# Adjacency counts of a graph network's first layer: six products in a row instead of four, one-hots asked for two batches ahead

## The chip, the cores and the metric

The kernel runs on one core of one Trainium2 chip. The metric is the device time of one launch in microseconds (us). Three runs of the kernel before gave 2123.55, 2127.40 and 2129.25 us; their median is 2127.4 us.

## The reference

A graph network of four layers over 6250 nodes with 256 channels and 100,000 edges, which come sorted by destination.

```python
h = jnp.maximum(_layernorm(x, axis=-1), 0.0)
# agg(h): for every node, the sum of h[src] over the edges that end in it
def agg(h):
    return jax.ops.segment_sum(h[src], dst, num_segments=N)
# ref(h): three layers of the first form, then the head (256 -> 256 -> 64 -> 256)
for l in range(NL - 1):
    h = x + agg(x)
    h = jax.nn.relu(h @ W1s[l] + b1s[l])
    h = jax.nn.relu(h @ W2s[l] + b2s[l])
    x = h @ W3s[l] + b3s[l]
...
return x + ref(h)
```

The sum over edges is a product with a 6250 x 6250 matrix of counts (how many edges run from node s to node d).

## The kernel before

The nodes lie in 49 blocks of 128. For 19 or so of the destination blocks the sum over edges is made by **gathering**: rows of a table in device memory are fetched by indirect DMAs (`rows`, issued by GpSimd) and added up by TensorE with one-hot matrices (`sums`, L1446). For the other 30 blocks the kernel builds the matrix of counts once, in the first layer, keeps it in device memory as bytes (`mat`), and multiplies with it in every layer: in the first layer `agg` at L1622 takes the counts straight from the build, in the later layers `agg` at L1700 reads them back.

**The build.** A block of 128 destinations is built in two halves of 16 sub-blocks each, so the 30 blocks have 960 sub-blocks. For one sub-block TensorE makes one product, `bp` (L1094), of two one-hot matrices of its edges: `lo` (the source's low seven bits, 128 columns, loaded as weights) and `hi` (the source's block and the destination within the sub-block, 196 columns, streamed). The one-hots are made by VectorE (helper `one_hot`, L1053) for a **batch** of four sub-blocks at a time, `lo` first and then `hi`; the pools hold two `lo` and two `hi` tiles (`bufs=2`). Before that ScalarE spreads the edges' numbers of a half block (`pairs`, L1048). A **step** of the generator `build` makes two products into one of three PSUM tiles `bp` and one copy of both into the block's counts `at`: the odd steps copy on ScalarE (L1102), the even ones on VectorE (L1104). So a batch is two steps: its first copy is ScalarE's, its second VectorE's. At a block's end VectorE adds the identity (L1108) and SyncE stores the block.

**The order of the work.** Instructions go to each engine's queue in the order in which the program writes them, and an engine takes its queue in order. The first 24 steps run before any product with counts. After that the loop `product_by_node` goes through **ticks**. In a tick it first runs what is due (results of the small layers, sums of gathered rows, VectorE's additions `u`, `un`, `zz`, the gathering's one-hots `hot`), then asks the build for some steps, then lets ScalarE cast counts for a later tick (`a`, L1582), and then issues four `agg` products. How many steps a tick asks for stands in a list `goals`, worked out ahead so that 480 steps are spread evenly over the layer:

```python
g0, u1 = GSUB + EARLY, steps - len(node_parts[-1]) - AHEAD - 1
goals = [min(g0 + (total - g0) * u // u1, total) for u in range(1, steps + 1)]
goals = [g - g % 2 for g in goals]
...
goal = min(goals[at - PRE], built[0] + 3)
while built[0] < goal and free_of(built[0] // GSUB - 3):
    next(beside)
    built[0] += 1
```

The goals are about one and a half steps a tick; rounded down to even numbers they come out as none or two steps in a tick. I call what TensorE does for one tick's steps a **piece**: two steps are a piece of four products.

Of the kernel before, what the change touches and what calls it, by code (L numbers as in the profile page):

```python
# [396 lines left out]
def sorted_edges(  # L397
# [55 lines left out]
    BATCH = 4  # L453
# [527 lines left out]
    with tc.manual_schedule():  # L981
# [61 lines left out]
        def pair(hots, k):  # L1043

            if k < len(batches):
                s = batches[k][0]
                pairs[s] = hots.tile([P, 2, GSUB, 2], BF16, name="pairs", bufs=3)
                nc.scalar.copy(pairs[s], clT[:, :, :, s - S0, None].to_broadcast([P, 2, GSUB, 2]))  # L1048

        def one_hot(o, values, which, n):  # L1050

            shape = [P, BATCH, n // 2, 2]
            nc.vector.tensor_tensor(  # L1053
                o.rearrange("p q (n t) -> p q n t", t=2),
                values.rearrange("p (n t) -> p n t", t=2)[:, None, :, :].to_broadcast(shape),
                which[:, :, None, :].to_broadcast(shape), OP.is_equal)

        def low_hot(hots, k):
            if k < len(batches):
                s, q0 = batches[k]  # L1060
                lo = hots.tile([P, BATCH, P], BF16, name="lo", bufs=2)
                one_hot(lo, lanes, pairs[s][:, 1, q0:q0 + BATCH, :], P)
                hot[k] = [lo]

        def high_hot(hots, k):
            if k < len(batches):
                s, q0 = batches[k]
                hi = hots.tile([P, BATCH, HW], BF16, name="hi", bufs=2)
                one_hot(hi, cols, pairs[s][:, 0, q0:q0 + BATCH, :], HW)
                hot[k].append(hi)  # L1070

        def build(hots, ats, ps_b):


            each = GSUB // BATCH
            pair(hots, 0)
            low_hot(hots, 0)
            high_hot(hots, 0)
            step = 0
            for k, (s, q0) in enumerate(batches):  # L1080
                b, half = divmod(s, 2)
                if half == 0 and q0 == 0:
                    at = counts[b] = ats.tile([P, NT, P], U8, name="at", bufs=3)
                lo, hi = hot.pop(k)
                if q0 == 0:
                    pair(hots, k + each)
                for q in range(0, BATCH, 2):
                    if q == 0:
                        low_hot(hots, k + 1)
                    elif q == 2:  # L1090
                        high_hot(hots, k + 1)
                    bp = ps_b.tile([P, W], F32, name="bp")
                    for m in range(2):
                        mm = nc.tensor.matmul(bp[:, m * HW:(m + 1) * HW], lo[:, q + m, :],  # L1094
                                              hi[:, q + m, :], start=True, stop=True)
                    passed(BUILD, mm)
                    d = half * 64 + (q0 + q) * GD
                    o = at[:, :, d:d + 2 * GD].rearrange("p h (i d) -> p h i d", i=2)
                    v = bp[:, :2 * HW].rearrange("p (i h d) -> p h i d", i=2, d=GD)
                    step += 1  # L1100
                    if step % 2 or step <= 2 * PRE:
                        nc.scalar.copy(o, v)  # L1102
                    else:
                        nc.vector.tensor_copy(o, v)  # L1104
                    if half and q0 + q + 2 == GSUB:
                        p, i = place_of[b]
                        own = at[:, b, :]
                        nc.vector.tensor_tensor(own, own, ident, OP.add)  # L1108
                        nc.sync.dma_start(out=mats[p][:, :, i, :],
                                          in_=at.rearrange("p (k h) d -> p k (h d)", h=CH))  # L1110
                    yield
# [449 lines left out]
        def passed(t, ins=None):  # L1561

            clock[0] += t
            if ins is not None:
                paced[:] = [ins.ins.name]
                for g in layers:
                    g.flow()
# [152 lines left out]
        total = GSUB * len(made)  # L1720
        steps = sum(map(len, node_parts))
        g0, u1 = GSUB + EARLY, steps - len(node_parts[-1]) - AHEAD - 1
        goals = [min(g0 + (total - g0) * u // u1, total) for u in range(1, steps + 1)]
        goals = [g - g % 2 for g in goals]
        built = [0]
        late = None
        ahead = ctx.enter_context(tc.tile_pool(name="ahead", bufs=1))
        with tc.tile_pool(name="hots", bufs=1) as hots, tc.tile_pool(
            name="ats", bufs=1
        ) as ats, tc.tile_pool(name="rings", bufs=AHEAD + 2) as rings, tc.tile_pool(  # L1730
            name="gath", bufs=24
        ) as gath, tc.tile_pool(
            name="ps_a", bufs=2, space=PSUM
        ) as ps_a, tc.tile_pool(name="ps_b", bufs=3, space=PSUM) as ps_b:
            begun = {0: clock[0]}
            rings.tile([P, 64], U8, name="align", bufs=1)
            layers[0].begin()
            layers[0].send(8)
            beside = build(hots, ats, ps_b)
            while now[0] < PRE:  # L1740
                for _ in range(2):
                    next(beside)
                    built[0] += 1
                tick(layers[0])
                layers[0].advance()
            later(1, lambda: later(2, lambda bad=verdict(): judge(bad)))
            for team in teams:
                product_of_team(*team, ps_a, beside, team == teams[-1])
            assert next(beside, None) is None and built[0] == total
# [15 lines left out]
def kernel(  # L1765
# [26 lines left out]
    good = keep.tile([1, 1], I32, name="good")  # L1792
    rest = (x, src, dst, W1s, b1s, W2s, b2s, W3s, b3s, cW1, cb1, cW2, cb2, cW3, cb3, out)
    sorted_edges(tc, good, *rest)
    done = nc.values_load(good[0:1, 0:1], min_val=0, max_val=1)
    with tc.If(done == 0):
# [27 lines left out]
```

## Time and profile before

| | |
|---|---|
| median of three runs | 2127.4 us |
| the profiled execution, its own time | 2128.08 us |
| its span, first to last instruction | 2126.3 us |
| TensorE busy / mean granted clock | 2034.3 us (96%) / 0.990 |
| VectorE, ScalarE, GpSimd busy | 925.0, 872.8, 1445.9 us |
| first layer's products with counts and the build beside them | about 134 to 640 us of the span |
| products `bp` | 960, on TensorE for 128.3 us |

The profile comes from one execution that took 2128.08 us by the same clock as the three runs. Times in the rows are in us from the start of the span unless marked ns. A row names line, engine and operation, what is written and read (`out<-in`), how often, and in brackets the idle time just before it with what ended it.

### The profile page before, as it was taken

The numbers are of one execution on the slowest core, as the hardware profiler recorded it, in microseconds if no ns is written. First come the engines' busy times: TensorE is split into PE (matmuls) and PEld (weight loads), VectorE is DVE, ScalarE is ACT, GpSimd is POOL, SyncE is SP. The second block draws the span as 40 slices with busy tenths as digits, with TensorE's granted clock in tenths as the row PEclk, the third lists the DMA queues.
The fourth block names the chain that finished last, engine by engine and source line by source line (L and its number), as shares of the span: only waits on it lengthen the run. The fifth ranks groups of instructions, "written<-read, shape, count | busy, mean of one in ns | idle before, by whom it ended". The sixth has DMA issues, their size and how long they took to land.

```text
span 2126.3 us, 33236 instructions
## 1 busy us (share of the span) xinstructions
PE 2034.3 (96%) x12076; PEld 1495.9 (70%) x12076; DVE 925.0 (44%) x2103; ACT 872.8 (41%) x1793; POOL 1445.9 (68%) x1467
## 2 busy tenths in 40 slices
PE   6889999999999999999999999999999999989998
PEld 4657676667676777777777777777776767766665
DVE  6987767677662422232234322322233323223333
ACT  5766656456555433323233423232233322222222
POOL 3747777677774477777777477777776477777772
PEclk9989999999999999999999999999999999999999
DMA  5534455545455654555566554555555555555563
GB/s 174 159 117 148 145 156 150 157 139 162 140 161 168 205 163 145 160 177 161 154 184 202 171 165 149 176 166 158 169 171 176 173 170 185 161 184 185 154 189 109
DMA packets 184900, 347.54 MB, mean 163 GB/s; under 512 B 32446, under 2 KB 118496, under 8 KB 184726
## 3 DMA queue, kind: packets, MB, share of 16 engines
q0 software_dynamic: 68960, 185.36, 29.9%
q1 hardware_dynamic: 113838, 158.12, 22.8%
q8 instruction: 96, 1.57, 0.3%
q10 hardware_dynamic: 1928, 1.85, 0.3%
q14 instruction: 78, 0.64, 0.1%
HBM read 287.93 MB, written 57.26 MB: 162 GB/s over the span
## 4 chain that ended last, share of the span: by engine, by line
PE 86%; DMA 4%; DVE 3%; issue 1%; ACT 1%; POOL 1%; DVEq 0%; SPq 0%; POOLq 0%; ACTq 0%
PE agg L1700 43%; PE agg L1622 15%; PE sums L1446 11%; PE ps L1256 6%; PE ps L1313 6%; PE bp L1094 4%; DMA rows<-table,idx 4%; PE ps L1506 1%; DVE hi L1053 1%; POOL rows L1407 1%; DVE at L1104 1%; PE ps L1268 1%; PE ps L1248 0%; DVE lo L1053 0%; ACT at L1102 0%
## 5 line engine op out<-in xcount | busy, mean ns | idle before, releaser
L1407 POOL DMA_INDIRECT rows<-table,idx x1394 | 1388.8, 996 | 595.7 <-issue 225.7
L1700 PE MATMUL agg<-a,XY 128*128 128x512 f32 x4116 | 978.6, 395 | 1.9 <-DVE clT L1634 1.9
L1700 PEld LDWEIGHTS agg<-a,XY 128*128 128x128 f32 x4116 | 764.9, 188 | 192.7 <-issue 35.0
L1598 ACT CAST a<-at 128x512 fp32r<-128x512 uint8 (+1 forms) x542 | 328.7, 617 | 653.7 <-PE agg L1700 613.1
L1598 DVE CAST a<-at 128x512 fp32r<-128x512 uint8 x543 | 246.8, 456 | 515.7 <-PE agg L1700 479.1
L1622 PE MATMUL agg<-XY,a 128*128 128x512 f32 x1470 | 405.4, 410 | 1.7 <-ACT a L1582 1.0
L1622 PEld LDWEIGHTS agg<-XY,a 128*128 128x128 f32 x1470 | 260.0, 190 | 51.4 <-issue 6.6
L1446 PE MATMUL sums<-rows,hot 128*32 128x256 f32 x3772 | 248.3, 391 | 33.5 <-DMA rows<-table,idx 33.3
L1446 PEld LDWEIGHTS sums<-rows,hot 128*32 128x32 f32 x3772 | 124.0, 111 | 151.0 <-DMA rows<-table,idx 46.1
L1582 ACT CAST a<-at 128x512 fp32r<-128x512 uint8 (+2 forms) x362 | 197.2, 576 | 6.6 <-PE agg L1622 6.6
L1102 ACT CAST at<-bp 128x392 uint8<-128x392 f32 x252 | 121.5, 490 | 186.9 <-PE bp L1094 181.3
L1104 DVE CAST at<-bp 128x392 uint8<-128x392 f32 x228 | 128.6, 564 | 137.4 <-PE bp L1094 135.0
L1475 DVE TENSOR_TENSOR u<-u,sums 128x256 f32<-128x256 f32 x82 | 34.4, 419 | 301.3 <-PE agg L1700 273.6
L1094 PE MATMUL bp<-hi,lo 128*128 128x196 bf16 x960 | 128.3, 256 | 14.9 <-DVE hi L1053 13.3
L1313 PE MATMUL ps<-w,h 128*128 128x256 f32 x588 | 133.8, 379 | 1.4 <-ACT h L1259 0.9
L1053 DVE TENSOR_TENSOR hi<-cols,pairs 128x784 bf16<-128x784 bf16 x240 | 134.9, 562 | 0.0
L1256 PE MATMUL ps<-h,w 128*128 128x512 f32 (+3 forms) x332 | 133.8, 545 | 0.3 <-ACT h L1713 0.3
L1094 PEld LDWEIGHTS <-lo 128*128 128x128 bf16 x960 | 72.3, 100 | 83.5 <-DVE hi L1053 34.9
L1313 PEld LDWEIGHTS ps<-w,h 128*128 128x128 f32 x588 | 111.3, 190 | 18.5 <-ACT h L1259 1.4
L1321 DVE TENSOR_TENSOR zz<-ps,w 128x512 f32<-128x512 f32 (+1 forms) x75 | 50.2, 679 | 116.5 <-PE ps L1313 116.5
L1053 DVE TENSOR_TENSOR lo<-lanes,pairs 128x512 bf16<-128x512 bf16 x240 | 100.6, 419 | 0.7 <-issue 0.3
L1510 ACT ACTIVATE h<-ps,bias 128x256 f32<-128x256 f32 (+1 forms) x116 | 47.6, 464 | 128.5 <-PE ps L1506 128.5
(170 smaller groups left out, 962.6 us busy)
## 6 DMA issues: line engine op xcount, KB each, us to landing
at<-mat SPq DMA_DIRECT2D x151, 448.0 KB
mat<-at SPq DMA_DIRECT2D x30, 784.0 KB
rows<-table,idx POOLq DMA_INDIRECT x1394
table<-zz SPq DMA_DIRECT2D x72, 256.0 KB
back<-table SPq DMA_DIRECT2D x99, 128.0 KB
xs<-in_x_dram SPq DMA_DIRECT2D x8, 768.0 KB
table<-zs SPq DMA_DIRECT2D x24, 256.0 KB
out_dram<-zz SPq DMA_DIRECT2D x24, 256.0 KB
```

Of the source, the lines that this page charges most:

```text
L1053: nc.vector.tensor_tensor(o.rearrange("p q (n t) -> p q n t", t=2), values.rearrange("p (n t) -> p n t", t=2)[:, None, :, :].to_broadcast( ...
L1094: mm = nc.tensor.matmul(bp[:, m * HW:(m + 1) * HW], lo[:, q + m, :], hi[:, q + m, :], start=True, stop=True)
L1102: nc.scalar.copy(o, v)
L1104: nc.vector.tensor_copy(o, v)
L1256: mm = nc.tensor.matmul(ps[:mp, :w], weights[l][0][:, c, i * P:i * P + mp], h1[:, c, :w], start=(c == 0), stop=(c == KC - 1))
L1313: mm = nc.tensor.matmul(o, h2[0][:, c, nodes], w3[:, c, :], start=(c == 0), stop=(c == KC - 1))
L1407: got = nc.gpsimd.indirect_dma_start(out=t, out_offset=None, in_=tables[self.l][:, :], in_offset=bass.IndirectOffsetOnAxis(ap=idx[:, o:o + ...
L1446: nc.tensor.matmul(self.sums[m * Q:(m + 1) * Q, :C], self.hot[:, c - min(rounds), m, :], self.rows[g, c + 4 * m], start=(c == ROUNDS[0][0] ...
L1582: nc.scalar.copy(a[:, i * m * P:(i + 1) * m * P].rearrange("p (j d) -> p j d", j=m), counts[b][:, j:j + m, :])
L1598: cast(o, at[:, :, d:d + m * P])
L1622: mm = nc.tensor.matmul(agg, a[:, d:d + P], XY[:, j, :], start=(j == 0), stop=(j == NT - 1))
L1700: mm = nc.tensor.matmul(agg[c][:, :w], XY[:, j, o:o + P], a[:, :w], start=(at == 0 and half == 0), stop=(at == NT - 1 and half == 1))
```

## The change

Three edits in the first layer's build. `goals` are rounded down to multiples of three instead of two (the last goal stays the full number), so a tick asks for three steps or none: a piece is six products. The two one-hots of batch k+2 are written behind the second step of batch k, where before those of batch k+1 were written ahead of batch k's first and second step; and the one-hots of the first two batches are written at the start instead of those of the first alone. The pools of `lo`, `hi`, `bp` and `at` keep their sizes. In the changed kernel L1094 is L1091, L1102 is L1099 and L1104 is L1101; L1053 and L1108 keep their numbers.

```diff
             each = GSUB // BATCH
             pair(hots, 0)
-            low_hot(hots, 0)
-            high_hot(hots, 0)
+            for k in range(2):
+                low_hot(hots, k)
+                high_hot(hots, k)
             step = 0
             for k, (s, q0) in enumerate(batches):
                 b, half = divmod(s, 2)
...
                 lo, hi = hot.pop(k)
                 if q0 == 0:
                     pair(hots, k + each)
                 for q in range(0, BATCH, 2):
-                    if q == 0:
-                        low_hot(hots, k + 1)
-                    elif q == 2:
-                        high_hot(hots, k + 1)
                     bp = ps_b.tile([P, W], F32, name="bp")
                     for m in range(2):
                         mm = nc.tensor.matmul(bp[:, m * HW:(m + 1) * HW], lo[:, q + m, :],
                                               hi[:, q + m, :], start=True, stop=True)
                     passed(BUILD, mm)
...
                     step += 1
                     if step % 2 or step <= 2 * PRE:
                         nc.scalar.copy(o, v)
                     else:
                         nc.vector.tensor_copy(o, v)
+                    if q + 2 == BATCH:
+                        low_hot(hots, k + 2)
+                        high_hot(hots, k + 2)
                     if half and q0 + q + 2 == GSUB:
                         p, i = place_of[b]
                         own = at[:, b, :]
                         nc.vector.tensor_tensor(own, own, ident, OP.add)
...
-        goals = [g - g % 2 for g in goals]
+        goals = [g if g == total else g - g % 3 for g in goals]
```

**TensorE's order**, right behind the first 24 steps (`bp`, `lo` and `hi` carry numbers, so that the tiles can be told apart). Before, a piece of four products and the `agg` of one tick:

```order
L1094 LDWEIGHTS lo_1440
L1094 MATMUL bp_1472<-hi_1446,lo_1440 128x196
L1094 LDWEIGHTS lo_1440
L1094 MATMUL bp_1472<-hi_1446,lo_1440 128x196
L1094 LDWEIGHTS lo_1440
L1094 MATMUL bp_1478<-hi_1446,lo_1440 128x196
L1094 LDWEIGHTS lo_1440
L1094 MATMUL bp_1478<-hi_1446,lo_1440 128x196
L1622 MATMUL agg_1453<-XY_71,a_1458 128x512 x4
```

Now the first piece of six there; eight `agg` stand ahead of it and eight behind it:

```order
L1091 LDWEIGHTS lo_1440
L1091 MATMUL bp_1482<-hi_1442,lo_1440 128x196
L1091 LDWEIGHTS lo_1440
L1091 MATMUL bp_1482<-hi_1442,lo_1440 128x196
L1091 LDWEIGHTS lo_1440
L1091 MATMUL bp_1486<-hi_1442,lo_1440 128x196
L1091 LDWEIGHTS lo_1440
L1091 MATMUL bp_1486<-hi_1442,lo_1440 128x196
L1091 LDWEIGHTS lo_1452
L1091 MATMUL bp_1494<-hi_1454,lo_1452 128x196
L1091 LDWEIGHTS lo_1452
L1091 MATMUL bp_1494<-hi_1454,lo_1452 128x196
```

A piece of four used one batch (`lo_1440`); a piece of six uses one and a half, and it fills all three `bp` tiles. The next piece begins with the second half of `lo_1452`. I call a piece that begins with a fresh batch an **A piece** and one that begins halfway a **B piece**; they alternate.

**VectorE's order**, some 410 us into the span, where the gathering's instructions fall between two pieces. Before:

```order
L1104 COPY at<-bp 128x49x8
L1475 TENSOR_TENSOR u<-u,sums 128x256
L1430 TENSOR_TENSOR hot<-colf,rel 128x768
L1634 TENSOR_TENSOR un<-un,agg 128x256
L1053 TENSOR_TENSOR lo<-lanes,pairs 128x512
L1053 TENSOR_TENSOR hi<-cols,pairs 128x784
L1104 COPY at<-bp 128x49x8
```

Now, at the same place:

```order
L1101 COPY at<-bp 128x49x8
L1053 TENSOR_TENSOR lo<-lanes,pairs 128x512
L1053 TENSOR_TENSOR hi<-cols,pairs 128x784
L1108 TENSOR_TENSOR at<-at,ident 128x128
L1475 TENSOR_TENSOR u<-u,sums 128x256
L1430 TENSOR_TENSOR hot<-colf,rel 128x768
L1634 TENSOR_TENSOR un<-un,agg 128x256
L1101 COPY at<-bp 128x49x8
```

The sequence of a batch's copy and the next one-hots (copy, `lo`, `hi`, copy, `lo`, `hi`) is the same in both kernels. What moved is the other work: it stood between a copy and the one-hots behind it, and stands now behind these one-hots and ahead of the next copy.

Counted over the layer behind the first 24 steps, TensorE's order had 224 pieces (216 of four products, 8 of six) and has 156 (148 of six, 4 of four, 4 of two). Between a B piece and the A piece behind it there stand 37 times exactly eight `agg`, 9 times five, and otherwise eight with further work (transposes L1506, the small layers L1256 and L1313, `sums` L1446) or more. The order of the later layers' instructions did not change.

## The prediction

> **What bounds the kernel now.** I read first the busy time by stage, then the chain of work that ended last, then who waited for whom in the first layer, then the timeline of single pieces. The stages (TensorE, its weight loads, VectorE, ScalarE and GpSimd busy, the granted clock, the DMA share):
>
> ```profile
> 121.00:134.00 13.00, 10.01 (x50) 5.48 (x50) 11.84 (x29) 10.42 (x27) 8.44 (x8) 0.50 0.58 192
> 134.00:640.00 506.00, 496.90 (x3356) 350.98 (x3357) 359.43 (x815) 302.79 (x683) 362.88 (x362) 0.99 0.49 148
> ```
>
> The first row is the build of the first 24 steps alone; the second is the stage that the change reorders. TensorE is busy for 496.9 of its 506 us, VectorE for 359, so on average nobody but TensorE binds. The chain says the same of the whole span:
>
> ```profile
> PE 86%; DMA 4%; DVE 3%; issue 1%; ACT 1%; POOL 1%; DVEq 0%; SPq 0%; POOLq 0%; ACTq 0%
> ```
>
> So a change in this stage is worth what it adds to or takes from TensorE's line: its own work, and its waits. The waits of TensorE from 134 to 640 us (total, times, longest):
>
> ```profile
> PE bp L1094 <- DVE hi L1053: 7.2, 12, 1.4
> PE agg L1622 <- ACT a L1582: 1.0, 1, 1.0
> PE ps L1313 <- ACT h L1510: 0.5, 1, 0.5
> PE bp L1094 <- ACT at L1102: 0.3, 2, 0.2
> ```
>
> Nearly all of it is a piece that waits for a one-hot `hi`. These waits are few, twelve of 224 pieces. The longest has VectorE's other work for a cause: behind a copy came `u`, `hot` and `un`, and only then the next one-hots.
>
> ```profile
> 407.82 1.17 PE L1622 MATMUL agg<-XY,a 128*128 128x512 f32 x4
> 410.34 0.26 PE L1094 MATMUL bp<-hi,lo 128*128 128x196 bf16 x1 [1.35 <-DVE hi L1053]
> ```
>
> **What the change can remove.** (1) These waits. Idle time is counted from a matmul's modelled end, but the next matmul may start earlier, so more is lost than the row says. One `agg` has a record of 413 ns, while twelve in a row take 2.79 us, 0.233 us each:
>
> ```profile
> L1622 PE MATMUL agg<-XY,a 128*128 128x512 f32 x1162 | 329.3, 413 | 1.0 <-ACT a L1582 1.0
> 327.71 2.79 PE agg L1622 x12
> ```
>
> Each wait costs 0.413 - 0.233 = 0.18 us more than its idle time. So the one-hots cost 7.2 + 12 x 0.18 = 9.4 us and the wait for ScalarE's copy 0.3 + 2 x 0.18 = 0.7 us. If the one-hots were truly ahead, 10.1 us would go.
>
> (2) Changes between the build's products and `agg`. The timeline has pieces of six and of four side by side, since the kernel before makes a few of six when it catches up:
>
> ```profile
> 438.78 0.67 PE L1094 MATMUL bp<-hi,lo 128*128 128x196 bf16 x6
> 439.24 1.17 PE L1622 MATMUL agg<-XY,a 128*128 128x512 f32 x4
> 440.25 0.34 PE L1094 MATMUL bp<-hi,lo 128*128 128x196 bf16 x2
> 440.76 0.51 PE L1094 MATMUL bp<-hi,lo 128*128 128x196 bf16 x4 [0.16 <-ACT at L1102]
> 441.05 1.18 PE L1622 MATMUL agg<-XY,a 128*128 128x512 f32 x4
> 442.07 0.51 PE L1094 MATMUL bp<-hi,lo 128*128 128x196 bf16 x4
> 442.37 0.48 PE L1622 MATMUL agg<-XY,a 128*128 128x512 f32 x1
> 443.35 0.51 PE L1094 MATMUL bp<-hi,lo 128*128 128x196 bf16 x4 [0.50 <-DVE hi L1053]
> ```
>
> Six products take 439.24 - 438.78 = 0.46 us, four take 0.29 or 0.30. Four `agg` between pieces take 1.01 us instead of 4 x 0.233 = 0.93, so each piece costs 0.08 us beside its products. Twelve products cost 3 x (0.30 + 0.08) = 1.14 us in fours and 2 x (0.46 + 0.08) = 1.08 us in sixes: about 0.05 us saved for each piece less (0.03 with 0.29). There are 224 - 156 = 68 fewer: 3.4 us (2 to 4).
>
> (3) In the first 24 steps VectorE's identity addition waits for ScalarE and holds up a one-hot behind it; it now stands behind that one-hot. The wait there was 0.70 us:
>
> ```profile
> 130.81 1.65 PE L1094 MATMUL bp<-hi,lo 128*128 128x196 bf16 x8 [0.70 <-DVE hi L1053]
> ```
>
> I take 0.5 us of it, between 0 and 0.7. The rest of that phase keeps its sequence.
>
> Together 9.4 + 0.7 + 3.4 + 0.5 = 14.0 us.
>
> **What it adds.** "Two batches ahead" gives less than it says. VectorE's sequence copy, `lo`, `hi`, copy is the same as before, and a batch's one-hots still go into the tiles of the batch two earlier: they cannot begin until that batch's last product is done. What changes is when TensorE wants them. A piece of six eats one and a half batches at once, and a B piece ends two batches. VectorE behind the pieces shown above:
>
> ```profile
> 439.32 0.57 DVE L1104 CAST at<-bp 128x392 uint8<-128x392 f32 x1 [2.26 <-PE bp L1094]
> 439.81 0.41 DVE L1053 TENSOR_TENSOR lo<-lanes,pairs 128x512 bf16<-128x512 bf16 x1
> 440.14 0.56 DVE L1053 TENSOR_TENSOR hi<-cols,pairs 128x784 bf16<-128x784 bf16 x1
> 440.63 0.57 DVE L1104 CAST at<-bp 128x392 uint8<-128x392 f32 x1
> 441.12 0.41 DVE L1053 TENSOR_TENSOR lo<-lanes,pairs 128x512 bf16<-128x512 bf16 x1
> 441.45 0.56 DVE L1053 TENSOR_TENSOR hi<-cols,pairs 128x784 bf16<-128x784 bf16 x1
> 441.93 0.56 DVE L1104 CAST at<-bp 128x392 uint8<-128x392 f32 x1
> 442.40 0.42 DVE L1053 TENSOR_TENSOR lo<-lanes,pairs 128x512 bf16<-128x512 bf16 x1
> 442.73 0.56 DVE L1053 TENSOR_TENSOR hi<-cols,pairs 128x784 bf16<-128x784 bf16 x1
> ```
>
> This is the new rhythm in small. The piece at 438.78 is an A piece: its second step's copy starts 0.54 us after it, and its one-hots let the product at 440.76 go, 1.98 us after it. At 440.25 products of the B kind begin (half a batch, then a batch). VectorE's copy starts 0.38 us after them; copy, `lo`, `hi` take 1.30 us, then the second copy, `lo`, `hi` follow without a break, and the product that needs the second `hi` starts at 443.35: **3.10 us after the B piece began.** Nothing else stood in VectorE's queue there and the copy cannot start before its products end, so 3.10 is a floor.
>
> When does TensorE want it? It is the second batch of the next A piece, its fifth product. The fifth starts 0.35 us into a piece (the last two of the six, from 439.13 on), and eight `agg` between two others take 311.28 - 309.34 = 1.94 us:
>
> ```profile
> 439.13 0.33 PE L1094 MATMUL bp<-hi,lo 128*128 128x196 bf16 x2
> 309.34 2.10 PE L1622 MATMUL agg<-XY,a 128*128 128x512 f32 x8
> 311.28 0.38 PE L1313 MATMUL ps<-w,h 128*128 128x256 f32 x1
> ```
>
> So it is wanted 0.46 + 1.94 + 0.35 = 2.75 us after the B piece began: a **wait of 0.35 us at every A piece that has just eight `agg` ahead of it**, 37 x 0.35 = 13.0 us. Where five `agg` stand there, the time is 3 x 0.233 = 0.70 us shorter and the wait 1.05 us: 9 x 1.05 = 9.5 us. Where a transpose, a small layer or sums stand there too, I take none. From A to B there is slack: the B piece's third product (0.18 us in, half of the fifth's 0.35) comes 0.46 + 1.94 + 0.18 = 2.58 us after the A piece began and its one-hots after 1.98. At four places pieces of two and four come with four `agg` between; there an A piece's one-hots are wanted after 0.46 + 1.01 + 0.18 = 1.65 us: 4 x 0.33 = 1.3 us.
>
> In the wait stand the rest of the piece and all `agg` behind it, so it adds to TensorE's line in full; the next copy waits with it, so the rhythm repeats instead of drifting.
>
> VectorE's other work comes on top where it falls ahead of a B piece. An A and a B piece together take 2 x 2.40 + 0.35 = 5.15 us, and three batches keep VectorE for 3.9 us; 1.25 us are free, enough for one `hot` of 0.95 us:
>
> ```profile
> L1430 DVE TENSOR_TENSOR hot<-colf,rel 128x768 f32<-128x768 f32 x21 | 20.0, 952 | 0.0
> ```
>
> So most of it fits, as it did not in the single batch between two pieces of four. I take 2 us for what does not, between 0 and the 9.4 us that it costs now.
>
> The three `bp` tiles are all filled by a piece; the last copy of a B piece starts 441.93 - 440.25 = 1.68 us after it began, long before 2.75: no wait. The store of a block moves behind two one-hots, under 1 us, ticks before its next use: nothing. The later layers keep their order, and the chain there is TensorE's and the gathering's; what the first layer loses shifts them whole.
>
> **The sum.** Added 13.0 + 9.5 + 1.3 + 2.0 = 25.8 us, removed 14.0: **+11.8 us.** On the profiled execution's 2128.1 us that is 2139.9; the median of the runs is 0.7 lower: **2139 us.**
>
> A rule of the Trainium skill bears on this ("Perfetto Trace Analysis", Optimization Strategy): the same gap repeating on the engine that should be saturated can mean that no buffer is free for the next tile. By it the repeated wait would be cured by a third pair of `lo` and `hi`, which this change does not bring; the trace shows twelve scattered waits and no regular one, so it has nothing to say of the kernel before.
>
> **The rivals.**
>
> *The one-hots are in time* (faster). Removed 14.0, nothing added: 2113 to 2116. For it: the longest waits now come from work that the change moves behind the one-hots. Against it: the 3.10 us. It wants the eight `agg` at least 0.35 us longer than measured. Chance 0.10.
>
> *Half of the wait is hidden* (no change). If ScalarE's casts `a` hold `agg` back between pieces, as once for 1.0 us in the waits above, the wait for the one-hot falls into that time. With half, 22.5 / 2 + 1.3 + 2.0 - 14.0 = +0.6 us: 2128, with 2124 to 2133 around it. Chance 0.17.
>
> *VectorE falls behind* (slower still). If the 1.25 us are not free when `hot` comes, each of the 21 adds its 0.95 us to a tight piece: 18 us more than I took, 2157. It decides where more than 1.25 us of other work stands ahead of a B piece. Chance 0.10.
>
> *The clock drops* (slower). In the first 24 steps TensorE was busy for 10.0 of 13 us and the granted clock was 0.50; with waits of 1.35 us in the stage behind it was 0.99. If the regular waits took a tenth of the 506 us to half clock, that tenth would last twice as long: +50 us, 2190. TensorE would then idle 0.35 of 5.15 us, far less than the 3 of 13. Chance 0.03. The Trainium skill ("TensorE: Matmul & The Clock Gate", A second HAM failure mode: psum-queue depth-cycling) tells of a kernel whose short idle times between groups made the clock swing between full and half; the trace's 0.99 speaks against it here.
>
> **How the numbers follow.** My forecast has 0.60; its own range is 2132 (waits of eight `agg` at half) to 2147 (other work at its upper bound). The range 2127 to 2150 leaves out the faster rival, the clock, and most of the falling behind, together 0.2. About 0.3%, 6.4 us, is what a measurement can tell from no change. Slower by more: 0.60 less a tenth of it, and 0.13, and a little of the half-hidden case: 0.69. Within: 0.20. Faster: 0.11.
>
> **What would show it.** Right: in the changed profile an idle of some 0.2 us (0.35 less 0.18 or so) in front of a piece's last two products, by `hi`, about every second piece, and 3.1 us from a B piece to them; `bp`'s idle by `hi` well above 7.2 us; waits of over 1 us rarer than before. Wrong: pieces of six without a break, or a stage from 134 us on that ends before 640; or waits that ScalarE's copies end.

## The result and the profile after

The changed kernel takes 2140.93 us (median of six runs, 2135.43 to 2143.27), the kernel before beside it 2126.97 us (six runs, 2123.44 to 2129.34): a ratio of 1.0064, 95% interval 1.0048 to 1.0081. That is 14.0 us slower; the forecast was +11.8 us, 2139. In the changed kernel the copies of a step stand at L1099 (ScalarE) and L1101 (VectorE) and the build's product at L1091. Not used below are one execution of the fifth experiment (2287.86 us, granted clock 0.848) and two single executions, 2400.78 us for the changed kernel and 2391.22 for the one before, from a chip on which all of them, a further one of the kernel before at 2377.9 included, took some 12% longer.

The chain of work that ended last, in the changed kernel, shares of the span by engine:

```profile
PE 81%; DVE 8%; DMA 4%; issue 1%; ACT 1%; POOL 0%; DVEq 0%; SPq 0%; POOLq 0%; ACTq 0%
```

VectorE has 8% of the chain instead of 3%, and TensorE 81% instead of 86%: the chain now leaves TensorE at many places and goes through VectorE. TensorE's waits from 134 to 655 us in the same execution (total, times, longest):

```profile
PE bp L1091 <- DVE hi L1053: 16.4, 47, 0.8
PE agg L1622 <- ACT a L1582: 1.0, 1, 1.0
PE ps L1506 <- ACT h L1259: 0.5, 1, 0.5
PE bp L1091 <- ACT at L1099: 0.3, 2, 0.2
```

Twelve scattered waits for `hi` have become 47, and none is over 0.8 us. Two pieces of the timeline, TensorE first (start, duration, instructions, and in brackets the idle time ahead and who ended it), with eight `agg` and with five between them:

```profile
144.11 0.69 PE L1091 MATMUL bp<-hi,lo 128*128 128x196 bf16 x6
144.58 2.09 PE L1622 MATMUL agg<-XY,a 128*128 128x512 f32 x8
146.51 0.52 PE L1091 MATMUL bp<-hi,lo 128*128 128x196 bf16 x4
147.21 0.34 PE L1091 MATMUL bp<-hi,lo 128*128 128x196 bf16 x2 [0.18 <-DVE hi L1053]
...
149.27 0.69 PE L1091 MATMUL bp<-hi,lo 128*128 128x196 bf16 x6
149.73 1.40 PE L1622 MATMUL agg<-XY,a 128*128 128x512 f32 x5
151.08 0.51 PE L1091 MATMUL bp<-hi,lo 128*128 128x196 bf16 x4
152.37 0.34 PE L1091 MATMUL bp<-hi,lo 128*128 128x196 bf16 x2 [0.77 <-DVE hi L1053]
```

And VectorE in the same timeline:

```profile
144.50 0.57 DVE L1101 CAST at<-bp 128x392 uint8<-128x392 f32 x1 [1.02 <-PE bp L1091]
144.98 0.41 DVE L1053 TENSOR_TENSOR lo<-lanes,pairs 128x512 bf16<-128x512 bf16 x1
145.31 0.56 DVE L1053 TENSOR_TENSOR hi<-cols,pairs 128x784 bf16<-128x784 bf16 x1
145.79 0.56 DVE L1101 CAST at<-bp 128x392 uint8<-128x392 f32 x1
146.26 0.42 DVE L1053 TENSOR_TENSOR lo<-lanes,pairs 128x512 bf16<-128x512 bf16 x1
146.60 0.56 DVE L1053 TENSOR_TENSOR hi<-cols,pairs 128x784 bf16<-128x784 bf16 x1
...
150.46 0.56 DVE L1053 TENSOR_TENSOR hi<-cols,pairs 128x784 bf16<-128x784 bf16 x1
```

The B piece at 144.11 runs without a break. VectorE, which had waited 1.02 us, starts its copy 0.39 us after it and then works copy, `lo`, `hi`, copy, `lo`, `hi` without a break; the product that needs the second `hi` starts at 147.21, **3.10 us after the B piece began**. The next B piece at 149.27 and its product at 152.37: again 3.10.

The stage from 134 us on (TensorE, its weight loads, VectorE, ScalarE, GpSimd busy, granted clock, DMA share), and the first and last start of the first layer's and the later layers' `agg` (durations min/median/max, then the two starts), after:

```profile
134.00:655.00 521.00, 502.93 (x3371) 356.88 (x3371) 357.90 (x816) 304.08 (x691) 363.07 (x365) 1.00 0.49 146
```

```profile
L1622 PE MATMUL agg<-XY,a x1470: 387/395/793, 134.6 to 1938.9; 128*128 128x512 f32 x184
L1700 PE MATMUL agg<-a,XY x4116: 387/389/796, 702.2 to 2131.1; 128*128 128x512 f32 x196
```

The same two rows of the kernel before:

```profile
L1622 PE MATMUL agg<-XY,a x1470: 387/395/799, 134.6 to 1923.5; 128*128 128x512 f32 x184
L1700 PE MATMUL agg<-a,XY x4116: 387/389/793, 690.8 to 2116.0; 128*128 128x512 f32 x196
```

The granted clock in this stage was 1.00. I take the time from the first L1622 to the first L1700 as the first layer's: 702.2 - 134.6 = 567.6 us after, 690.8 - 134.6 = 556.2 before, **+11.4 us**. The span after is 2141.5 us, so what follows takes 1439.3 us, before 2126.3 - 690.8 = 1435.5. Whether these other 3.8 us belong to the change is asked in the last experiment.

### The profile page after: what moved, and what is told of

Read it like the earlier page. It is cut to its first block, busy times and chain, and to the rows that moved or that the text cites. A ratio compares the mean times of both kernels' runs of the same rounds, so it can differ in the third digit from the quotient of the medians.

```text
span 2141.5 us, 33241 instructions
## 1 busy us (share of the span) xinstructions
PE 2040.3 (95%) x12076; PEld 1501.4 (70%) x12076; DVE 920.5 (43%) x2103; ACT 870.8 (41%) x1793; POOL 1444.5 (67%) x1467
## 4 chain that ended last, share of the span: by engine, by line
PE 81%; DVE 8%; DMA 4%; issue 1%; ACT 1%; POOL 0%; DVEq 0%; SPq 0%; POOLq 0%; ACTq 0%
PE agg L1700 42%; PE agg L1622 11%; PE sums L1446 11%; PE ps L1313 6%; PE ps L1256 6%; DMA rows<-table,idx 4%; PE bp L1091 3%; DVE hi L1053 2%; DVE at L1101 2%; DVE lo L1053 2%; PE ps L1506 1%; PE ps L1268 1%; ACT at L1099 0%; PE ps L1248 0%; DVE hot L1430 0%
## 5 line engine op out<-in xcount | busy, mean ns | idle before, releaser
L1700 PE MATMUL agg<-a,XY 128*128 128x512 f32 x4116 | 979.0, 395 | 1.9 <-DVE clT L1634 1.9
L1700 PEld LDWEIGHTS agg<-a,XY 128*128 128x128 f32 x4116 | 765.1, 188 | 193.1 <-issue 35.1
L1622 PE MATMUL agg<-XY,a 128*128 128x512 f32 x1470 | 391.5, 406 | 1.7 <-ACT a L1582 1.0
L1622 PEld LDWEIGHTS agg<-XY,a 128*128 128x128 f32 x1470 | 262.7, 189 | 59.7 <-issue 10.7
L1446 PE MATMUL sums<-rows,hot 128*32 128x256 f32 x3772 | 249.9, 393 | 33.6 <-DMA rows<-table,idx 33.3
L1446 PEld LDWEIGHTS sums<-rows,hot 128*32 128x32 f32 x3772 | 124.7, 112 | 151.9 <-DMA rows<-table,idx 45.9
L1099 ACT CAST at<-bp 128x392 uint8<-128x392 f32 x252 | 119.1, 489 | 191.6 <-PE bp L1091 185.1
L1101 DVE CAST at<-bp 128x392 uint8<-128x392 f32 x228 | 128.3, 563 | 157.9 <-PE bp L1091 154.9
L1582 ACT CAST a<-at 128x512 fp32r<-128x512 uint8 (+2 forms) x362 | 191.0, 576 | 9.2 <-PE agg L1622 9.2
L1091 PE MATMUL bp<-hi,lo 128*128 128x196 bf16 x960 | 124.6, 255 | 23.3 <-DVE hi L1053 21.5
L1313 PE MATMUL ps<-w,h 128*128 128x256 f32 x588 | 135.4, 383 | 0.9 <-ACT h L1259 0.9
L1053 DVE TENSOR_TENSOR hi<-cols,pairs 128x784 bf16<-128x784 bf16 x240 | 134.8, 562 | 0.0
L1256 PE MATMUL ps<-h,w 128*128 128x512 f32 (+3 forms) x332 | 133.8, 545 | 0.3 <-ACT h L1713 0.3
L1091 PEld LDWEIGHTS <-lo 128*128 128x128 bf16 x960 | 71.8, 99 | 82.9 <-DVE hi L1053 39.0
L1313 PEld LDWEIGHTS ps<-w,h 128*128 128x128 f32 x588 | 112.6, 192 | 18.3 <-ACT h L1259 1.3
L1053 DVE TENSOR_TENSOR lo<-lanes,pairs 128x512 bf16<-128x512 bf16 x240 | 100.2, 417 | 0.7 <-issue 0.5
```

Of the source, the lines that this page charges most:

```text
L1053: nc.vector.tensor_tensor(o.rearrange("p q (n t) -> p q n t", t=2), values.rearrange("p (n t) -> p n t", t=2)[:, None, :, :].to_broadcast( ...
L1256: mm = nc.tensor.matmul(ps[:mp, :w], weights[l][0][:, c, i * P:i * P + mp], h1[:, c, :w], start=(c == 0), stop=(c == KC - 1))
L1313: mm = nc.tensor.matmul(o, h2[0][:, c, nodes], w3[:, c, :], start=(c == 0), stop=(c == KC - 1))
L1446: nc.tensor.matmul(self.sums[m * Q:(m + 1) * Q, :C], self.hot[:, c - min(rounds), m, :], self.rows[g, c + 4 * m], start=(c == ROUNDS[0][0] ...
L1582: nc.scalar.copy(a[:, i * m * P:(i + 1) * m * P].rearrange("p (j d) -> p j d", j=m), counts[b][:, j:j + m, :])
L1622: mm = nc.tensor.matmul(agg, a[:, d:d + P], XY[:, j, :], start=(j == 0), stop=(j == NT - 1))
```

## The experiments

The theory: the batch's one-hots are too late by a fixed amount, because VectorE's sequence from a B piece to the second `hi` behind it takes 3.10 us and TensorE wants that `hi` earlier; fours did not have this, and making one-hots earlier cannot cure it with two pairs of tiles. The rivals: sixes alone cost nothing and the new place of the one-hots costs; the tiles alone are short; ScalarE could hide it; the first trace is an odd one.

**Sixes alone** (kernel before with the new goals):

```diff
-        goals = [g - g % 2 for g in goals]
+        goals = [g if g == total else g - g % 3 for g in goals]
```

> Pieces of six products, but the one-hots written where the kernel before writes them (one batch ahead). My theory (the waits come from the piece of six: a B piece ends two batches, and VectorE's copy, lo, hi, copy, lo, hi has its last hi ready 3.10 us after the piece began, while it is wanted after 2.75 us, or 2.05 where five agg stand between): the same waits of 0.35 us and about 1.0 us stay, and other work of VectorE comes between a copy and the one-hots again, so 0 to 6 us slower than the changed kernel, ratio to the kernel before 1.006 to 1.010. Rival (writing the one-hots further ahead is what costs): the loss is gone, ratio 0.997 to 1.001.

Measured 2169.83 us, ratio 1.019 (1.0172 to 1.0208): the direction was right, the size not, it is far slower than the changed kernel. TensorE's waits for `hi` from 134 to 690 us:

```profile
PE bp L1094 <- DVE hi L1053: 41.6, 56, 2.1
```

With 0.18 us more for each that is 41.6 + 56 x 0.18 = 51.7 us instead of 9.4. One such wait in this kernel's timeline, both engines:

```profile
173.15 0.56 DVE L1104 CAST at<-bp 128x392 uint8<-128x392 f32 x1
173.28 0.51 PE L1094 MATMUL bp<-hi,lo 128*128 128x196 bf16 x4
...
173.62 0.41 DVE L1475 TENSOR_TENSOR u<-u,sums 128x256 f32<-128x256 f32 x1
...
173.95 0.95 DVE L1430 TENSOR_TENSOR hot<-colf,rel 128x768 f32<-128x768 f32 x1
...
174.82 0.41 DVE L1053 TENSOR_TENSOR lo<-lanes,pairs 128x512 bf16<-128x512 bf16 x1
175.15 0.56 DVE L1053 TENSOR_TENSOR hi<-cols,pairs 128x784 bf16<-128x784 bf16 x1
...
175.77 0.34 PE L1094 MATMUL bp<-hi,lo 128*128 128x196 bf16 x2 [1.97 <-DVE hi L1053]
```

In the old order the one-hots of a batch are written only when the batch ahead of it starts, that is behind the tick's `u` and `hot`; here these put 174.82 - 173.62 = 1.20 us between the copy and the one-hots, and the wait, already tight, grows by that. It is no single case: in this trace some thirty of the waits have `u`, `hot`, `un` or `zz` in VectorE's line ahead of the `hi`, and they hold about 34 of the 41.6 us. So the two edits do not add up: sixes without the earlier one-hots cost 42 us, and with them 14.

**One-hots ahead alone** (changed kernel with the old goals):

```diff
-        goals = [g if g == total else g - g % 3 for g in goals]
+        goals = [g - g % 2 for g in goals]
```

> Pieces of four products as before, the one-hots written two batches ahead. My theory: the sequence copy, lo, hi is the same and a batch is used at a time, so no regular wait; some of the twelve waits behind u, hot, un, zz go: 0 to 7 us faster than the kernel before, ratio 0.9965 to 1.000, idle of bp by hi 2 to 6 us instead of 7.2. Rival (writing them ahead is what costs, since copies and the identity addition now wait behind them or they hold up u and un): ratio about 1.006.

Measured 2122.77 us, ratio 0.998 (0.9967 to 0.9994), with these waits for `hi` from 134 to 655 us:

```profile
PE bp L1091 <- DVE hi L1053: 5.1, 11, 1.3
```

The earlier one-hots are a small gain by themselves, 4 us by the ratio (1 to 7 by its interval). They do not take the scattered waits away: 5.1 + 11 x 0.18 = 7.1 us of the 9.4 are left, the longest still 1.3 us. There, at 409.41, VectorE had worked `u`, `hot`, `un`, copy, `lo`, `hi` without a break: the other work that stood ahead of the one-hots stands now ahead of the copy, and the one-hots behind that copy are late all the same. The loss is in the sixes.

**Three pairs of tiles, three batches ahead** (changed kernel; two row tiles fewer in the first layer's pool make room):

```diff
-                lo = hots.tile([P, BATCH, P], BF16, name="lo", bufs=2)
+                lo = hots.tile([P, BATCH, P], BF16, name="lo", bufs=3)
...
-                hi = hots.tile([P, BATCH, HW], BF16, name="hi", bufs=2)
+                hi = hots.tile([P, BATCH, HW], BF16, name="hi", bufs=3)
...
-            for k in range(2):
+            for k in range(3):
...
-                        low_hot(hots, k + 2)
-                        high_hot(hots, k + 2)
+                        low_hot(hots, k + 3)
+                        high_hot(hots, k + 3)
...
-            name="gath", bufs=24
+            name="gath", bufs=22
```

> Pieces of six, three lo and three hi tiles, one-hots written three batches ahead; to make room the first layer's gathering has 22 row tiles instead of 24. My theory: in a B piece the one-hots wanted by the next A piece's fifth product now stand behind the first copy, ready 1.82 us after the piece began, wanted at 2.75: the regular waits go, about 22 to 26 us faster than the changed kernel, ratio to the kernel before 0.994 to 0.997. Rival (VectorE simply has too much work in this stage): the waits stay in sum, ratio 1.004 or more. Rival (the loss lies in the later layers): ratio about 1.006.

Measured 2116.11 us, ratio 0.9942 (0.9923 to 0.9961): faster than both kernels. No wait for `hi` is left among the waits from 134 to 655 us; the build's products wait only for ScalarE's copies:

```profile
PE bp L1091 <- ACT at L1099: 1.3, 3, 0.5
```

TensorE's timeline shows A and B pieces alike, unbroken:

```profile
141.10 0.68 PE L1091 MATMUL bp<-hi,lo 128*128 128x196 bf16 x6
141.57 2.11 PE L1622 MATMUL agg<-XY,a 128*128 128x512 f32 x8
143.52 0.68 PE L1091 MATMUL bp<-hi,lo 128*128 128x196 bf16 x6
```

And its first and last starts:

```profile
L1622 PE MATMUL agg<-XY,a x1470: 387/395/797, 133.0 to 1911.8; 128*128 128x512 f32 x184
L1700 PE MATMUL agg<-a,XY x4116: 387/389/796, 677.7 to 2100.2; 128*128 128x512 f32 x196
```

The first layer takes 677.7 - 133.0 = 544.7 us, 11.5 less than before. This is the prediction's faster rival, brought about: it was priced at 2113 to 2116.

**Three pairs, still two ahead** (the same without the three lines that write further ahead):

```diff
-                lo = hots.tile([P, BATCH, P], BF16, name="lo", bufs=2)
+                lo = hots.tile([P, BATCH, P], BF16, name="lo", bufs=3)
...
-                hi = hots.tile([P, BATCH, HW], BF16, name="hi", bufs=2)
+                hi = hots.tile([P, BATCH, HW], BF16, name="hi", bufs=3)
...
-            name="gath", bufs=24
+            name="gath", bufs=22
```

> The changed kernel with three lo and three hi tiles, still two batches ahead, 22 row tiles in the first layer. My theory: the tiles are free when VectorE comes to them, its queue is what is late, so nothing changes: ratio to the kernel before 1.005 to 1.008, the same waits of 0.35 us. Rival (a repeated gap means that no buffer is free for the next tile): the waits go, ratio about 0.995. If 22 row tiles cost something, it shows here too.

Measured 2138.28 us, ratio 1.0046 (1.0029 to 1.0063), which overlaps the changed kernel's interval. Its waits for `hi`, from 134 to 655 us:

```profile
PE bp L1091 <- DVE hi L1053: 15.5, 45, 0.8
```

A free tile alone is worth almost nothing: the batch's one-hots still stand behind the same copy in VectorE's queue, and the copy behind the same products. The rule of the Trainium skill that the prediction weighed ("Perfetto Trace Analysis", Optimization Strategy: a gap that repeats on the engine that should be saturated can mean too few buffers) is half of the answer here: with the third pair but the old order 15.5 us of waits stayed, and only with both were they gone. No cost of the two row tiles given up shows in this run.

**One-hots ahead of the copy** (changed kernel, the same place in the program but in the other order):

```diff
+                    if q + 2 == BATCH:
+                        low_hot(hots, k + 2)
+                        high_hot(hots, k + 2)
                     step += 1
                     if step % 2 or step <= 2 * PRE:
                         nc.scalar.copy(o, v)
                     else:
                         nc.vector.tensor_copy(o, v)
-                    if q + 2 == BATCH:
-                        low_hot(hots, k + 2)
-                        high_hot(hots, k + 2)
```

> The changed kernel with the one-hots of batch k+2 written ahead of the second step's copy instead of behind it. My theory: in a B piece VectorE then goes lo, hi, copy, lo, hi, copy. The second hi lets its product go 2.63 us after the piece began, in time for 2.75, but the last copy ends only some 3.1 us after it, and the next A piece's third step needs that copy's bp tile at 2.75: the wait stays at about 0.35 us and changes its name to VectorE's copy. Ratio to the kernel before 1.003 to 1.008, bp's idle by hi well below the 16.4 us of the changed kernel and by the copy L1104 or its like well above 0. Rival (only the one-hots are late): the 37 waits go, ratio about 1.000.

Measured 2139.65 us, ratio 1.0056 (1.0035 to 1.0076), and the waits from 134 to 655 us (in this kernel L1102 is ScalarE's copy and L1104 VectorE's):

```profile
PE bp L1091 <- ACT at L1102: 8.2, 16, 0.8
PE bp L1091 <- DVE at L1104: 6.4, 28, 0.6
...
PE bp L1091 <- DVE hi L1053: 0.5, 1, 0.5
```

The wait for `hi` is gone and the time stays: the copies that free the three `bp` tiles are now last. With 0.18 us for each of the 45 waits the three rows hold 15.1 + 8.1 = 23.2 us, against 16.4 + 47 x 0.18 = 24.9 in the changed kernel. The same operations in another order are late by about as much, while one operation less, in the next experiment, is not late behind eight `agg`. That ScalarE's copies would be charged with 8.2 of the 15.1 us was not expected. One such wait, in a piece that began at 153.87:

```profile
154.40 0.50 ACT L1102 CAST at<-bp 128x392 uint8<-128x392 f32 x1
154.65 0.56 DVE L1104 CAST at<-bp 128x392 uint8<-128x392 f32 x1
154.94 0.33 PE L1091 MATMUL bp<-hi,lo 128*128 128x196 bf16 x2 [0.56 <-ACT at L1102]
```

The fifth product starts while VectorE's copy still runs, and 0.04 us after the end of ScalarE's, which is the copy of the same piece's first step. All 16 follow the first step's copy in this way. That points to the first step's tile and not, as expected, to the one that the piece before filled last; why the tile would come from there is not shown.

**One copy of three given to ScalarE** (changed kernel; of a batch's VectorE copies, the one of each B piece's first step, whose `lo` and `hi` are the first in the tight sequence):

```diff
-                    if step % 2 or step <= 2 * PRE:
+                    if step % 2 or step % 6 == 4 or step <= 2 * PRE:
```

> The changed kernel with the first copy of every B piece on ScalarE instead of VectorE, so VectorE goes lo, hi, copy, lo, hi there. My theory: the second hi lets its product go 2.63 us after the piece began instead of 3.10: the 37 waits of 0.35 us go and the 9 with five agg fall from 1.05 to about 0.6, 17 us less; ScalarE gets 76 copies of 0.49 us more in a stage where it is busy for 304 of 521 us and gives back up to 5. Ratio to the kernel before 0.997 to 1.002. Rival (ScalarE becomes the bound of the stage): casts a come late, ratio 1.005 or more, agg idle by ScalarE.

Measured 2122.62 us, ratio 0.9989 (0.9976 to 1.0003). The waits from 134 to 655 us, and then the timeline of TensorE:

```profile
PE bp L1091 <- DVE hi L1053: 5.0, 13, 0.7
```

```profile
148.44 2.10 PE L1622 MATMUL agg<-XY,a 128*128 128x512 f32 x8
150.38 0.68 PE L1091 MATMUL bp<-hi,lo 128*128 128x196 bf16 x6
150.85 1.41 PE L1622 MATMUL agg<-XY,a 128*128 128x512 f32 x5
152.09 0.52 PE L1091 MATMUL bp<-hi,lo 128*128 128x196 bf16 x4
153.01 0.34 PE L1091 MATMUL bp<-hi,lo 128*128 128x196 bf16 x2 [0.40 <-DVE hi L1053]
```

One copy less in the 3.10 us (0.48 us from its start to that of `lo`) is enough behind eight `agg`: the piece at 150.38 is whole. Behind five it is not: 153.01 - 152.09 = 0.92 us instead of 0.35, a wait of 0.57. ScalarE took 76 copies more (every sixth step behind the first 24, in which all copies are its own). TensorE waits for it no longer than before: 1.0 us for `a`, 0.5 for `h`, 0.3 for the copies, as in the changed kernel. VectorE's waits for ScalarE rose from 0.7 to 9.4 us, but the total does not show them. So the margin is as computed, a few tenths of a microsecond.

**Three pairs, three ahead, in fours** (the third experiment's kernel with the old goals):

```diff
-        goals = [g if g == total else g - g % 3 for g in goals]
+        goals = [g - g % 2 for g in goals]
```

> Pieces of four, three lo and three hi tiles, one-hots three batches ahead, 22 row tiles in the first layer: the kernel with pieces of six and the same (ratio 0.9942) with only the piece's size put back. My theory: the twelve waits behind other work go (up to 10 us), the saving of the larger piece (68 changes at 0.05 us, 3.4 us) is missing: ratio to the kernel before 0.994 to 0.998, last bp product 2 to 5 us later after the first agg than with sixes. Rival (all the gain of three ahead with sixes comes from the size): ratio 0.999 to 1.001.

Measured 2115.37 us, ratio 0.9943 (0.9924 to 0.9962), the same as in sixes within the intervals. Its starts:

```profile
L1622 PE MATMUL agg<-XY,a x1470: 387/396/797, 132.8 to 1912.3; 128*128 128x512 f32 x184
L1700 PE MATMUL agg<-a,XY x4116: 387/389/792, 680.1 to 2106.5; 128*128 128x512 f32 x196
```

The first layer takes 547.3 us, 2.6 more than in sixes. With no wait for a one-hot in either (the products wait for ScalarE's copies for 1.3 us in sixes and for 0.6 in fours), this is an estimate of what 68 changes between the build's products and `agg` are worth, about 0.04 us each. Since the first layer differs by up to 1.7 us between two traces of one kernel (last experiment), it may be 0.01 to 0.06; the time of the whole run does not show it.

**Second traces of both kernels**, to see what varies between executions (unchanged kernels). The expectations reckon the later layers to an earlier point, 7.0 us before the end: 1432.3 and 1428.5 us for the 1439.3 and 1435.5 above.

> The changed kernel once more, for a second trace that can be compared (the two before this took 12% longer for both kernels). If the 3.8 us of the later layers are the kernel's own, they take 1431 to 1434 us here too; if they differ from execution to execution, any time from 1425 to 1434. The first layer repeats: 567 to 568 us.

> The kernel before once more, for the same comparison: first layer 556 to 557 us; later layers 1428 to 1429 us if what they take is the kernel's own, else any time from 1425 to 1434.

Measured: 2138.59 us, ratio 1.0056 (1.0021 to 1.0092), span 2134.6, for the changed kernel; 2127.24 us, ratio 1.0002 (0.9989 to 1.0016), span 2129.2, for the one before. The starts in the changed kernel's second trace:

```profile
L1622 PE MATMUL agg<-XY,a x1470: 387/394/796, 134.3 to 1933.8; 128*128 128x512 f32 x184
L1700 PE MATMUL agg<-a,XY x4116: 387/389/793, 703.5 to 2124.4; 128*128 128x512 f32 x196
```

And in the second trace of the kernel before:

```profile
L1622 PE MATMUL agg<-XY,a x1470: 387/395/799, 134.1 to 1921.3; 128*128 128x512 f32 x184
L1700 PE MATMUL agg<-a,XY x4116: 387/389/793, 689.6 to 2118.8; 128*128 128x512 f32 x196
```

First layer 569.2 and 555.5 us, 1.2 and 0.5 us outside what was expected: +13.7, against +11.4 in the first pair of traces. What follows it takes 2134.6 - 703.5 = 1431.1 us after and 2129.2 - 689.6 = 1439.6 before, the other way round than at first (1439.3 and 1435.5); by the expectations' count that is 1424.1 and 1432.6, the first just below the 1425 to 1434 that were expected. So the later layers vary by 8 us from execution to execution with the same order, and the 3.8 us of the first trace are that; the loss lies in the first layer.

## Why the prediction was right, point by point

**The floor of 3.10 us** was met to the hundredth, at 147.21 and at 152.37.

**Eight `agg` ahead: 0.35 us.** 147.21 - 146.51 = 0.70 us from the first product to the fifth instead of 0.35: a wait of 0.35. Of the 47 waits 27 are of this kind, in front of a fifth product behind eight `agg` and with 0.15 to 0.19 us of idle time; the forecast had 37. With 0.18 us for each they hold 9.7 us instead of 13.0.

**Five ahead: 1.05 us.** Eight of the nine places show 0.77 us of idle time; the ninth, at 341.55, shows 0.52. The one at 152.37 is 1.29 - 0.35 = 0.94 us late; the missing 0.11 lies in front of the piece: its first product started 151.08 - 149.73 = 1.35 us after the `agg` began, where five take 1.24 in the sixth experiment (152.09 - 150.85). It came 0.62 us after the start of the first `hi` at 150.46, as the fifth does after the second (147.21 - 146.60 = 0.61), so it waited too, unseen behind a modelled end. The eight hold 7.6 us by their idle time, 8.5 with this 0.11, where nine were put at 9.5.

**The other twelve** idle times, 0.16 to 0.75 us, add up to 5.3 us, or 7.5 with 0.18 each. Three stand at the small pieces; seven stand at a fifth product behind eight `agg`, where the wait is longer than 0.35 us. In nine of the twelve VectorE had `un`, `u`, `zz` or `hot` in its line shortly before. The forecast had 3.3 us for the small pieces and the other work together: here it was too low.

**Sum of what it adds:** 24.9 us by the waits, forecast 25.8. (The 0.18 us was taken from `agg`; in front of a fifth product the hidden part is 0.16 to 0.17, so the 24.9 may be up to a microsecond too high; the hidden 0.11 at eight places, which it leaves out, makes up for that.) The total fits better than its parts: the two regular kinds hold 4 to 5 us less than forecast and the rest 4 more, and that these cancel is luck.

**What it removes,** forecast 14.0 us. The twelve old waits of 9.4 us cannot be told from the new ones: the 24.9 us hold whatever is left of them. None of over 0.8 us is left, but the second experiment shows that the earlier one-hots alone took only 9.4 - 7.1 = 2.3 us of them, so the reason given, that the change moves the other work behind the one-hots, carries little in fours. For the sum it does not matter: the waits grew by 24.9 - 9.4 = 15.5 us. ScalarE's copy did not go: its row still reads 0.3, 2, 0.2, so the 0.7 us stayed. The fewer changes gave about 2.6 us (third and seventh experiment), forecast 3.4. The start, put at 0.5, gave nothing that shows: the first `agg` starts at 134.6 in both first traces, and at 134.3 and 134.1 in the second. So 15.5 - 2.6 = **+12.9 us**, between the +11.4 and +13.7 of the two pairs of traces; 14.0 by the medians.

**The rivals.** One-hots in time: fell at 3.10 us, and came true with a third pair written three ahead. Half hidden by ScalarE: fell, since `a` held `agg` up only once in both kernels, for 1.0 us. VectorE behind: not to its size here, though its other work cost more than was put for it; this is what sixes in the old order do, where the longest wait is 2.1 us. The clock: granted 1.00 in the stage, with 47 waits in it. The Trainium skill's case of short idle times that make the clock swing ("TensorE: Matmul & The Clock Gate", A second HAM failure mode: psum-queue depth-cycling) did not arise here with waits of 0.35 us about every 5 us.

**What the prediction had not seen** is how much the second edit is worth under the first. Alone it gains 4 us; beside the sixes it takes their loss from 42 us to 14.

## What to carry to other kernels

Before a piece is made bigger, follow the other engine's queue from the instruction that frees a tile to the one that fills it again, and set that time against the time until the bigger piece wants it: here 3.10 against 2.75 us decided, though VectorE was busy for only 69% of the stage. "Further ahead" needs both a free tile and a place further ahead in the producer's queue; a free tile alone left the wait where it was, and an earlier place alone (ahead of the copy) gave it another name. So when a wait disappears from the list, look at the total.

## What the runs showed of the hardware

With the same order of instructions, the part of the kernel behind the first layer took between 1431.1 and 1439.6 us in four executions, so a single trace cannot tell 4 us there; the first layer repeated within 2 us. A change between the build's bf16 products and the 512-column `agg` costs TensorE an estimated 0.01 to 0.06 us, from the 2.6 us between two kernels that are 68 such changes apart.
